# A convolution that adds its own input in the kernel tap, and predicated copies in place of masked adds

## The chip, the cores and the metric

The kernel runs on one core of one Trainium2 chip. A core has five engines, each with its own instruction stream: TensorE (PE, matrix products into the eight PSUM banks), VectorE (DVE), ScalarE (ACT), GpSimd (POOL) and SyncE (SP, which here mostly issues loads). They share the on-chip memory SBUF and meet through semaphores. The metric is the time of one execution on the device, in microseconds (us).

## The reference, cut to what matters

```python
# x: 32 x 64 x 1024 (batch, head or token, position or feature), float32
x = x + conv(x)        # per head: a causal convolution over 1024 positions with a kernel
                       # built from 64 states, plus x * D[head]; then zero behind length[batch]
x = x + einsum('bsi,boi->bso', x, weight1[ids1])     # per batch: its own 1024 x 1024 adapter
x = x + einsum('bij,bkj->bik', x, weight2[ids2])     # and a second one
gate = x @ Wg.T + low_rank(x, ids3)                  # 1024 -> 2752
up   = x @ Wu.T + low_rank(x, ids3)
x = x + (silu(gate) * up) @ Wd.T + low_rank(...)     # 2752 -> 1024
```

The convolution is `y = (k * u + u * D) * mask`, with `mask` one at the positions below the length of the batch and zero behind. So what goes on is `x + k*x + D*x` where the mask is one, and `x` itself where it is zero.

## The kernel before

**Layout.** The 32 batches are four chunks of eight (`NCK`, `BC`). `xs[c]` holds a chunk as 128 partitions by 8 feature tiles by 512 tokens. The convolution is computed for all four chunks at once, at the start. Its result for the first chunk goes into `xs[0]` in SBUF, that for the other three to a buffer `cd` in DRAM, from which `bring(c)` loads it later.

**The convolution** (`convolution`, about the first 140 us) handles 64 heads in 16 units of four; two units make a group, so there are eight groups g, and `period(g)` works on one. Inside it four streams run side by side, in an order that is written out by hand for DVE, ACT, POOL and SP (`period`, `run`, `spread`: a list of steps at which each piece is put among DVE's steps of the scan):

- ACT makes powers, 16 small products `m` for each unit (`products`, line 1602), in pieces of 8, 3 and 5 for one unit and 3 and 13 for the other; it also takes four results out of PSUM into SBUF (`xg<-pv`, line 1690), the turned powers (`e<-pt`, line 1664) and the taps (`ks<-pk`, line 1719).
- DVE sums the products into `zs` (two instructions for a unit, in `new_powers`), runs the scan over the states (`scan`: instructions `t` and `xg`), and takes the finished results out of the banks (`taken`). All DVE helpers go through `tt`, so their line is 1337.
- PE turns `zs` (`pt`), computes `pv` from it, the taps `pk`, and two parts of the result into the banks `py`: `direct` (from the taps) and `carried` (from the states, after the scan of that group has ended).
- The finished unit lies in two banks `py`, one for each `side`; each is 128 partitions by two heads by 4 chunks by 64. `taken` has three pieces: `masked(0)` and `masked(1)` multiply a whole bank by the mask into `tmp`, `added` adds the first chunk's part of `tmp` to `xs[0]` and stores the rest to `cd`.

The last group, g=7, has no further scan beside it. The banks are handed out in turn by `ps_tile`, eight in all, so a bank is used again eight allocations later.

**The adapters of the first chunk** follow, 16 of them (`adapter`, line 233). Their weights, 512 KB for each eighth of an adapter (k counts the eighths from 0), come through nine rotating buffers `w`, and 35 of them are `own`: loaded ahead into places in memory that the convolution leaves free, step by step (`places`, `fetch`: EARLY, then LATE, BETWEEN and LAST as groups end). `OWN_ENDS` says after how many adapters this memory is given up (`first.close()`), and `FIRST_RUN, RUN` which eighths are `own`. Between the adapters 10 and 13 stand small pieces of the next part: three `begin_rest(i)` (each loads one 512 KB block, runs eight matmuls and one ACT copy), and the first loads and products of the feed-forward part.

**The feed-forward part** (`ffn`) runs chunk by chunk, in three blocks, with sums of weights (`halves`, `quarters`, `sides`) that spare products. It loads `sums` and `parts` through the same nine buffers `w`, in order on SP's queue. The adapters of the next chunk are put between its pieces. `take(c)` adds the convolution's result to chunk c: eight DVE instructions of 128x512 (line 335) that `fill` hands out one by one, by an assumed cost, while the next chunk's first use of `xs[c]` is still to come.

Of the kernel before, what the change touches and what calls it, by code (L numbers as in the profile page):

```python
# [9 lines left out]
F32 = mybir.dt.float32  # L10
I32 = mybir.dt.int32
AF = mybir.ActivationFunctionType
ALU = mybir.AluOpType
# [6 lines left out]
P = 128  # L20
B, H, L = 32, 64, 1024
NS = 64
KT = L // P
NCK = 4
BC = B // NCK
TC = BC * H
# [6 lines left out]
MG = 2  # L33
NG = FM // MG
EARLY = 17
OWN_ENDS = 11
LATE = 5
BETWEEN = 4
LAST = 5
# [1 line left out]
WARM = 20  # L41
FIRST_ = 11
SECOND_ = 5
FIRST_RUN, RUN = 13, 11
MID = 6
ROTATING = 9
HA = 4
SEG = 2
TH = TC // 2
# [37 lines left out]
def kernel(  # L87
# [26 lines left out]
    nc = tc.nc  # L114
# [3 lines left out]
    wpool = ctx.enter_context(tc.tile_pool(name="wpool", bufs=ROTATING))  # L118
# [8 lines left out]
    def ps_tile(name):  # L127
        return psum.tile([P, 512], F32, tag="ps", name=name)

    cst = cpool.tile([P, CO_N], F32, tag="cst", name="cst")  # L130
# [11 lines left out]
    xs = [x_tile(0)]  # L142
    first = ExitStack()
# [6 lines left out]
    cd = dpool.tile([NCK - 1, P, H // HA, HA * KT * BC], F32, tag="cd", name="cd")  # L150
# [92 lines left out]
    def first_sides():  # L243


        for layer, b in list(layers(0))[:2]:
            acc, wts = begun[layer, b] = ps_tile(f"pa{layer}_{b}"), []
            for kt in range(KT if b == 0 else SECOND_):
                wts.append(next(stream))
                adapter_part(acc, wts[kt], kt, b * H, 0)  # L250
                yield
# [33 lines left out]
                ALU.add,  # L285
            )

    g0 = convolution(tc, cst, consts, xt, xf, ssm, eye, lens, xs[0], cd, ps_tile, fetch, places, (row_ids, rows_now), first, first_sides())
    for _ in before:
        pass  # L290

# [4 lines left out]
    later = deque()  # L296
# [28 lines left out]
    def take(c):  # L325
        n, half = H // 4, KT * BC // 2
        for q in range(4):
            t = came.pop(q)
            for i in (0, 1):

                def add(q=q, t=t, i=i):
                    rows_ = slice(i * half, (i + 1) * half)
                    xv = xs[c].rearrange("p k (b h) -> p (k b) h", h=H)
                    xv = xv[:, rows_, q * n : (q + 1) * n]
                    nc.vector.tensor_add(xv, xv, t.rearrange("p i k -> p k i")[:, rows_])

                later.append((1.0, add))

# [2 lines left out]
    def adapters(c):  # L343
        for layer, b in layers(c):
            yield adapter(layer, b)

    def rest_tile(i, name):
        wt = wpool.tile([P, KT, P], F32, tag="w", name=f"wr{i}_{name}")
        load = nc.sync.dma_start(wt.rearrange("p k f -> p (k f)"), wr[i])
        return wt, load.ins  # L350

    def rest_part(c, wt, ps, t0, t1):

        tokens = slice(t0, t1)
        for kt in range(KT):
            nc.tensor.matmul(  # L356
                ps[:, tokens],
                wt[:, kt, :],
                xs[c][:, kt, tokens],
                start=(kt == 0),  # L360
                stop=(kt == KT - 1),
            )

    layers0 = adapters(0)
    for _ in range(OWN_ENDS):
        next(layers0)
    first.close()

# [1 line left out]
    hpool = ctx.enter_context(tc.tile_pool(name="hpool", bufs=1, reuse_waits="tile"))  # L370
    gpool = ctx.enter_context(tc.tile_pool(name="gpool", bufs=2, reuse_waits="tile"))
# [26 lines left out]
    sums = [dpool.tile([7, P, 4 * QP], F32, tag=f"sums{i}", name=f"sums{i}") for i in range(2 * NG)]  # L398
    parts = [dpool.tile([4, P, 3 * QP], F32, tag=f"parts{i}", name=f"parts{i}") for i in range(2 * NG)]
    cols = []  # L400

    def columns(table, c, n, name, tags=("raw", "at"), behind=None):

# [29 lines left out]
    tms = {}  # L433
    for name in "gu":
        tms[name] = hpool.tile([P, 2 * H], F32, tag=f"tm_{name}", name=f"tm_{name}")
    rest1 = hpool.tile([P, TC], F32, tag="rest1", name="rest1")
    rest2 = hpool.tile([P, 2, TH], F32, tag="rest2", name="rest2")

    def pair(j):
        return slice(2 * R * j, 2 * R * (j + 1))  # L440
# [231 lines left out]
    def quarters(c, gi, g, o, xb, _, early, also=lambda: None):  # L672

        name = f"{c}_{gi}_{g}"
# [6 lines left out]
        def load(js):  # L681
            bs, as_ = [], []

            def home(j, n, name):
                pool, tag, bufs = (gpool, "wy", 2) if j == 2 else (wpool, "w", ROTATING)
                return pool.tile([P, n, KQ, P], F32, tag=tag, name=name, bufs=bufs)

            for j in js:
                t = home(j, 3, f"wb{j}_{name}")
                src = wq[2 * gi + g, raw[j]] if j in raw else parts[2 * gi + g][at_parts[j]]  # L690
                nc.sync.dma_start(t.rearrange("p i k f -> p (i k f)"), src)
                bs.append(t)
            for j in js:
                if j == 0:
                    t = gpool.tile([P, 4, KQ, P], F32, tag="wx", name=f"wa{j}_{name}", bufs=1)
                else:
                    t = home(j, 4, f"wa{j}_{name}")
                nc.sync.dma_start(
                    t.rearrange("p i k f -> p (i k f)"), sums[2 * gi + g][at_sums[j]]
                )  # L700
                as_.append(t)

            return [
                [b[:, 0], b[:, 1], a[:, 3], b[:, 2], a[:, 0], a[:, 1], a[:, 2]]
                for a, b in zip(as_, bs)
            ]
# [69 lines left out]
        add = nc.vector.tensor_add  # L776
        c11, c12, c21, c22 = quarter(o)
        l11, l12, _, _ = quarter(lt)
# [185 lines left out]
    def ffn(c, xb, sides0, others):  # L964
# [39 lines left out]
        tv = None  # L1004
        for block, (m0, m1) in enumerate(BLOCKS):
# [65 lines left out]
                flush()  # L1071
            if c == 0 and last:
                phase.close()
                qpool[0] = ctx.enter_context(
                    tc.tile_pool(name="qpool1", bufs=1, side="right", reuse_waits="tile")
                )
# [15 lines left out]
            for h in range(KH):  # L1092
                name = f"{c}_{block}_{h}"
                if last and h > 1 and more_come:
                    prepare(c + 1, "gu"[h - 2], ready)
                banks = [ps_tile(f"po{j}_{name}") for j in range(4)]

                home = {0: 0, 5: 1, 6: 2, 4: 3, 1: 4, 3: 5, 2: 6}
                pss = [banks[home[j] // 2][:, home[j] % 2 * TH :][:, :TH] for j in range(7)]
                for s0 in range(m0, m1, SEG):  # L1100
# [3 lines left out]
                    if block == 0:  # L1104
                        w = [wl[:, h, i] for i in range(3)]
                        tails = {1: (w[0], 0), 3: (w[1], 0), 4: (w[1], 1), 2: (w[2], 1)}
                    elif end and last:
# [3 lines left out]
                        w = [[wl[:, t, i, h * P : (h + 1) * P] for i in (0, 1)] for t in (0, 1)]  # L1111
# [69 lines left out]
            store()  # L1181
        return steps[0] if more_come else None

    def begin_rest(i):
        wt, ps = rest_tile(i, "first")[0], ps_tile(f"pr{i}_first")
        rest_part(0, wt, ps, 0, TH)
        nc.scalar.copy((rest1, rest2[:, 0], rest2[:, 1])[i][:, :TH], ps[:, :TH])
        return wt

    places_ = act_tile(0, "first").rearrange("p i m t -> p i (m t)")  # L1190
    other_ = apool.tile([P, MG, 4, TH], F32, tag="actd", name="actd_first")
    weight_places = [
# [34 lines left out]
        first_weight(m, 0)  # L1227
    xb, part = first_moving()
    next(layers0)
    begin_rest(1)  # L1230
    next(layers0)
    part(0, 2)
    begin_rest(2)
    next(layers0)
    tables = [
        columns(ag, 0, KT, "g_0", behind=loads[-1]),
# [22 lines left out]
        sides0 = None  # L1259


def convolution(tc, cst, consts, xt, xf, ssm, eye, lens, x0, cd, ps_tile, fetch, places, rows_now, first, sides):

# [7 lines left out]
    nc = tc.nc  # L1273
    NG_ = len(PAIRS)
    with ExitStack() as ctx:
# [18 lines left out]
        def load_u(g):  # L1294
            for u in range(PAIRS[g] // 2):
# [14 lines left out]

        shape = [P, NCK, 2, 2, KT * BC]
        work = [
            g0.tile(shape, F32, tag="tmp", name=f"work{i}", bufs=2).rearrange(
                "p c j s e -> p (c j s e)"
            )
            for i in (0, 1)
# [19 lines left out]
        def tt(o, a, b, op):  # L1336
            nc.vector.tensor_tensor(o, a, b, op)  # L1337
            return o
# [223 lines left out]
        nc.gpsimd.dma_start(kps[:, :P], zero)  # L1562

        lnf = g0.tile([P, B], F32, tag="lnf", name="lnf")
        mask = g0.tile([P, NCK, KT, BC], F32, tag="mask", name="mask")
        maskf = mask.rearrange("p c k b -> p (c k b)")
        nc.gpsimd.tensor_copy(lnf, ln)

        powers = {}

# [241 lines left out]
        def taken(g, u, c0=0, c1=NCK):  # L1812


            i_ = first_unit[g] + u
            ha = i_ * HA

            def masked(side):
                if c0 == 0 and side == 0:
                    tmps[i_] = g0.tile(shape, F32, tag="tmp", name=f"tmp{i_}", bufs=2)  # L1820
                tt(
                    tmps[i_][:, c0:c1, :, side].rearrange("p c j e -> p j c e"),
                    banks[g, u][side].rearrange("p j (c e) -> p j c e", c=NCK)[:, :, c0:c1],
                    maskf.rearrange("p (c e) -> p c e", c=NCK)[:, c0:c1]
                    .unsqueeze(1)
                    .to_broadcast([P, 2, c1 - c0, KT * BC]),
                    ALU.mult,
                )

            def added():  # L1830
                tmp = tmps[i_]
                if c0 == 0:
                    xv = x0.rearrange("p k (b h) -> p k b h", h=H)[..., ha : ha + HA]
                    tv = tmp[:, 0].rearrange("p j s (k b) -> p k b (j s)", b=BC)
                    tt(xv, xv, tv, ALU.add)
                if c1 == NCK:
                    queue = nc.scalar if g >= NG_ - 3 else nc.sync
                    queue.dma_start(
                        cd.rearrange("c p g e -> p c g e")[:, :, i_],
                        tmp[:, 1:].rearrange("p c j s e -> p c (j s e)"),  # L1840
                    )

            return (lambda: masked(0)), (lambda: masked(1)), added

        def masks():
            nc.vector.tensor_tensor(
# [407 lines left out]
```

## Time and profile before

| | |
|---|---|
| times of three runs | 2229.07, 2229.59, 2232.77 us |
| the profiled execution | 2230.71 us |
| its span | 2229.1 us |
| TensorE clock granted | 0.998 |
| PE busy | 2190.1 us (98%) |
| DVE busy | 1370.6 us (61%) |
| ACT busy | 423.8 us (19%) |
| POOL busy | 207.3 us (9%) |
| moved by DMA | 656.35 MB, 294 GB/s |

The profiled execution is 1.12 us above the median of the three, and 1.6 us lie around its span. A line of the timeline gives the start, the time to the end of the last of its instructions, the engine, the line of the kernel, output<-inputs, the shape, and in brackets how long the engine was idle before and what ended that. Successive instructions overlap a little, so an instruction's share of its engine is the distance of two starts, somewhat less than its own duration. In a line of waits stand the total, the number and the longest.

### The profile page before, as it was taken

Reading aid. Unit: us, or ns where it says so; the run is one execution under the profiler, and the core shown is the slowest. Engines: PE = TensorE matmul, PEld = TensorE weight load, DVE = VectorE, ACT = ScalarE, POOL = GpSimd, SP = SyncE. Lnnn points to the kernel's source line nnn. Section 1 sums busy time; section 2 is a strip of 40 time slices with the busy share of each in tenths; the row PEclk is TensorE's granted clock in tenths of the full one; section 3 lists DMA queues with packets and bytes.
Section 4 is the critical chain, followed back from the end, with each engine's and each line's share of the span. In section 5 each row is a group of like instructions: output and inputs, shape, how many; then the busy total and the mean of one; then the engine's idle time right before and its main releaser. Section 6 shows DMA issues by size and latency. Waiting matters only on the chain.

```text
span 2229.1 us, 53636 instructions
## 1 busy us (share of the span) xinstructions
PE 2190.1 (98%) x21488; PEld 1806.0 (81%) x21488; DVE 1370.6 (61%) x2995; ACT 423.8 (19%) x1042; POOL 207.3 (9%) x328
## 2 busy tenths in 40 slices
PE   7999999999999999999999999999999999999999
PEld 5765687877787896888689897788688988899998
DVE  8961386675367766565346666466336666576675
ACT  6800120110011121121012212122002212121220
POOL 1010031111011210000000111000000011000000
PEclk9999999999999999999999999999999999999999
DMA  8899998899979558799979848799989938384681
GB/s 316 272 346 396 404 376 297 331 361 362 361 285 370 195 199 312 286 361 357 354 289 362 279 145 319 275 350 363 353 294 359 329 107 290 121 291 177 215 277 41
DMA packets 204683, 656.35 MB, mean 294 GB/s; under 512 B 24066, under 2 KB 40834, under 8 KB 203922
## 3 DMA queue, kind: packets, MB, share of 16 engines
q1 hardware_dynamic: 173122, 565.84, 69.4%
q0 software_dynamic: 23392, 76.07, 9.1%
q10 hardware_dynamic: 7920, 11.01, 1.4%
q8 instruction: 169, 2.77, 0.5%
q14 instruction: 80, 0.66, 0.1%
HBM read 585.66 MB, written 67.17 MB: 293 GB/s over the span
## 4 chain that ended last, share of the span: by engine, by line
PE 86%; DVE 6%; DMA 5%; issue 3%; POOL 0%; ACT 0%; SPq 0%; POOLq 0%; DVEq 0%; ACTq 0%
PE pq L717 29%; PE po L1127 24%; PE pa L233 17%; PE pf L611 7%; PE pr L356 3%; DMA wa<-in_w 3%; PE pe L478 2%; DVE xg L1337 1%; DVE t L1337 1%; DMA sums<-kept 1%; PE pl_d L449 1%; DVE tmp L1337 1%; DMA wr_first<-in_wr 1%; PE pr_first L356 0%; DVE zs L1337 0%
## 5 line engine op out<-in xcount | busy, mean ns | idle before, releaser
L233 PE MATMUL pa<-wa,x 128*32 128x256 f32 x7632 | 431.7, 380 | 9.0 <-DMA wa<-in_w 9.0
L717 PE MATMUL pq<-xd,wa 128*128 128x128 f32 x3360 | 414.9, 275 | 0.4 <-DMA wa<-sums 0.4
L717 PEld LDWEIGHTS pq<-xd,wa 128*128 128x128 f32 x3360 | 394.6, 192 | 0.7 <-DMA wa<-sums 0.5
L233 PEld LDWEIGHTS pa<-wa,x 128*32 128x32 f32 x7632 | 240.6, 110 | 183.4 <-DMA wa<-in_w 17.7
L717 PE MATMUL pq<-xd,wb 128*128 128x128 f32 x2520 | 323.6, 276 | 0.0
L717 PEld LDWEIGHTS pq<-xd,wb 128*128 128x128 f32 x2520 | 300.5, 192 | 3.6
L262 DVE STREAM_TRANSPOSE y<-pa 128x512 f32<-128x512 f32 x64 | 45.9, 717 | 270.7 <-PE pa L233 266.9
L1127 PE MATMUL po<-act,wd 128*128 128x256 f32 x640 | 168.6, 386 | 0.0
L1127 PE MATMUL po<-actd,wd 128*128 128x256 f32 x640 | 164.2, 379 | 0.0
L1127 PE MATMUL po<-actd,s 128*128 128x256 f32 x640 | 164.2, 379 | 0.0
L504 DVE TENSOR_TENSOR s<-wd 128x256 f32<-128x256 f32 x80 | 33.8, 422 | 177.6 <-PE po L1127 177.5
L1127 PEld LDWEIGHTS po<-act,wd 128*128 128x128 f32 x640 | 117.8, 190 | 29.3 <-issue 12.5
L611 PE MATMUL pf<-xd,wf 128*128 128x256 f32 x576 | 135.5, 381 | 0.0
L1159 ACT COPY uo<-po 128x256 f32<-128x256 f32 x48 | 17.9, 372 | 616.3 <-PE po L1127 606.3
L1127 PEld LDWEIGHTS po<-actd,wd 128*128 128x128 f32 x640 | 121.6, 190 | 16.5
L1127 PEld LDWEIGHTS po<-actd,s 128*128 128x128 f32 x640 | 121.6, 190 | 16.5
L375 POOL DMA_INDIRECT bgu<-in_bgu,rows x44 | 44.6, 1014 | 968.3 <-PE pe L478 826.4
L611 PEld LDWEIGHTS pf<-xd,wf 128*128 128x128 f32 x576 | 108.7, 190 | 15.5
L611 PE MATMUL pf<-xd,s 128*128 128x256 f32 x480 | 114.5, 382 | 1.1 <-DVE up L652 1.0
L741 ACT COPY u<-pq 128x256 f32<-128x256 f32 x120 | 41.5, 345 | 367.0 <-PE pq L717 310.5
L611 PEld LDWEIGHTS pf<-xd,s 128*128 128x128 f32 x480 | 90.2, 190 | 16.9 <-DVE up L652 2.9
L746 DVE TENSOR_TENSOR u<-u,u 128x256 f32<-128x256 f32 x120 | 46.6, 388 | 73.9 <-ACT u L743 73.9
(275 smaller groups left out, 2762.8 us busy)
## 6 DMA issues: line engine op xcount, KB each, us to landing
wa<-in_w SPq DMA_DIRECT2D x477, 512.0 KB
wa<-sums SPq DMA_DIRECT2D x210, 512.0 KB
wb<-parts SPq DMA_DIRECT2D x120, 384.0 KB
wd<-in_wd SPq DMA_DIRECT2D x80, 512.0 KB
wb<-in_wq SPq DMA_DIRECT2D x90, 384.0 KB
sums<-kept POOLq DMA_DIRECT2D x30, 1024.0 KB, 7.7
wf<-in_wu SPq DMA_DIRECT2D x20, 512.0 KB
early<-in_w SPq DMA_DIRECT2D x17, 512.0 KB
```

The costliest lines, as they stand in the source:

```text
L233: nc.tensor.matmul(acc[i * S : (i + 1) * S, s * 256 : (s + 1) * 256], xs[lo // TC][:, kt, lo % TC + s * S : lo % TC + (s + 1) * S], wt[:, ...
L262: nc.vector.transpose(y, acc)
L356: nc.tensor.matmul(ps[:, tokens], wt[:, kt, :], xs[c][:, kt, tokens], start=(kt == 0), stop=(kt == KT - 1),)
L375: nc.gpsimd.indirect_dma_start(out=t, out_offset=None, in_=table, in_offset=bass.IndirectOffsetOnAxis(ap=at_, axis=0),)
L478: nc.tensor.matmul(ps[:, at_ * 2 * H : (at_ + 1) * 2 * H], bt[pair(j), g], tms[table][pair(j)], start=(g == 0), stop=True, skip_group_chec ...
L504: nc.vector.tensor_add(s1, a21, a22)
L611: nc.tensor.matmul(ps, ws[j][:, kt, :], xb[j][:, kt, :], start=start and kt == 0, stop=kt == KH - 1, skip_group_check=True,)
L717: nc.tensor.matmul(ps[:, to * TQ : (to + 1) * TQ], w[i][:, k, :], xb[:, j, SLOT[i], k, :], start=start and k == 0 and to == 0, stop=k == K ...
L741: nc.scalar.copy(u, pa)
L746: nc.vector.tensor_add(u, v, u)
L1127: nc.tensor.matmul(pss[j], *term, start=(s0 == m0 and i == 0 and home[j] % 2 == 0), stop=(end and i == len(terms) - 1 and not late), skip_ ...
L1337: nc.vector.tensor_tensor(o, a, b, op)
```

## The change

1. **Convolution.** The skip weight `dskip` gets one added (one POOL instruction), so the tap at zero distance holds D+1 and the banks hold result plus input. `masked` and `added` give way to `chosen` and `stored`. For each side, a predicated copy on DVE writes the bank's first chunk (128 by 2 heads by 64) into `xs[0]` where the mask, read as integers, is not zero; a plain copy takes the other three chunks (128 by 384) into `tmp`. The copy of side 0 is on DVE in groups 0 to 5, that of side 1 on ACT; in groups 6 and 7 both are on ACT. What is stored in `cd` is no longer masked.
2. **`take(c)`.** Each of the 24 adds of line 335 becomes a predicated copy of the same 128x512, with the mask; the cost that `fill` assumes goes from 1.0 to 1.2.
3. **Order.** `OWN_ENDS` goes from 11 to 12, `RUN` from 11 to 8: the `own` eighths are k = 2, 5, 8, 11, 13 to 20 and then every third from 22 (before: 13 to 23, then every third from 25). `begin_rest(1)` and `begin_rest(2)` move before the adapters 10 and 11; `begin_rest(0)`, which stood after adapter 10, now stands after adapter 11.
4. **Memory.** A pool `home` lives to the end and holds the mask and the two `tmp` buffers, in whose places `rest1` and `rest2` (now one tile `rests`) come later. A pool `rpool` with two buffers `wz`, from chunk 1 on, takes two of the eleven loads of a `quarters` step that went through the nine buffers `w`.

```diff
-OWN_ENDS = 11
+OWN_ENDS = 12
-FIRST_RUN, RUN = 13, 11
+FIRST_RUN, RUN = 13, 8
...
+    home = ctx.enter_context(tc.tile_pool(name="home", bufs=1))
+    mask = home.tile([P, NCK, KT, BC], F32, tag="mask", name="mask")
...
-                nc.vector.tensor_add(xv, xv, t.rearrange("p i k -> p k i")[:, rows_])
-                later.append((1.0, add))
+                    nc.vector.copy_predicated(
+                        xv,
+                        mask[:, c].rearrange("p k b -> p (k b)").bitcast(I32)[:, rows_]
+                        .unsqueeze(2)
+                        .to_broadcast([P, half, n]),
+                        t.rearrange("p i k -> p k i")[:, rows_],
+                    )
+                later.append((1.2, choose))
...
     layers0 = adapters(0)
-    for _ in range(OWN_ENDS):
+    for i in range(OWN_ENDS):
+        if i > OWN_ENDS - 3:
+            begin_rest(i - OWN_ENDS + 3)
         next(layers0)
     first.close()
...
-                pool, tag, bufs = (gpool, "wy", 2) if j == 2 else (wpool, "w", ROTATING)
+                pool, tag, bufs = wpool, "w", ROTATING
+                if j == 2:
+                    pool, tag, bufs = gpool, "wy", 2
+                elif j == 1:
+                    pool, tag, bufs = rpool[0], "wz", 2
...
-        maskf = mask.rearrange("p c k b -> p (c k b)")
+        maski = mask.rearrange("p c k b -> p (c k b)").bitcast(I32)
         nc.gpsimd.tensor_copy(lnf, ln)
+        nc.gpsimd.tensor_scalar(dskip, dskip, 1.0, None, ALU.add)
...
-            def masked(side):
-                if c0 == 0 and side == 0:
-                    tmps[i_] = g0.tile(shape, F32, tag="tmp", name=f"tmp{i_}", bufs=2)
-                tt(
-                    tmps[i_][:, c0:c1, :, side].rearrange("p c j e -> p j c e"),
-                    banks[g, u][side].rearrange("p j (c e) -> p j c e", c=NCK)[:, :, c0:c1],
-                    maskf.rearrange("p (c e) -> p c e", c=NCK)[:, c0:c1]
-                    .unsqueeze(1)
-                    .to_broadcast([P, 2, c1 - c0, KT * BC]),
-                    ALU.mult,
-                )
-
-            def added():
-                tmp = tmps[i_]
-                if c0 == 0:
-                    xv = x0.rearrange("p k (b h) -> p k b h", h=H)[..., ha : ha + HA]
-                    tv = tmp[:, 0].rearrange("p j s (k b) -> p k b (j s)", b=BC)
-                    tt(xv, xv, tv, ALU.add)
+            def chosen(side):
+                if c0 == 0:
+                    h = ha + side
+                    nc.vector.copy_predicated(
+                        x0.rearrange("p k (b h) -> p h (k b)", h=H)[:, h : h + 3 : 2],
+                        maski[:, : KT * BC].unsqueeze(1).to_broadcast([P, 2, KT * BC]),
+                        bank[side][:, :, 0],
+                    )
+                if c1 == NCK:
+                    if side == 0:
+                        tmps[i_] = home.tile(shape, F32, tag="tmp", name=f"tmp{i_}", bufs=2)
+                    copy = nc.vector.tensor_copy if side == 0 and g < NG_ - 2 else nc.scalar.copy
+                    copy(
+                        tmps[i_][:, 1:, :, side].rearrange("p c j e -> p j c e"),
+                        bank[side][:, :, 1:],
+                    )
```

## The prediction

> **What bounds the kernel now.** First I read the busy shares and PE's waits by stretch: they give all that a change outside PE can win. In the waits a line holds who waited, for what, the total, the number, the longest.
>
> ```profile
> PE 2190.1 (98%) x21488; PEld 1806.0 (81%) x21488; DVE 1370.6 (61%) x2995; ACT 423.8 (19%) x1042; POOL 207.3 (9%) x328
> ```
> ```profile
> PE py L1797 <- DVE xg L1337: 6.6, 7, 1.6
> ...
> PE pa L233 <- DMA wa<-in_w: 3.8, 8, 1.3
> PE pr_first L356 <- DMA wr_first<-in_wr: 0.6, 2, 0.3
> ...
> PE pa L233 <- DMA wa<-in_w: 5.2, 7, 1.7
> ```
>
> The first is from 0 to 146 us, the next two from 146 to 300, the last from 300 on. PE idles only 39 us (2229.1 less 2190.1). In the convolution it loses 6.6 to DVE's scan; up to 300 it loses 4.4 to loads. The table by stretch says what limits there (length, PE, PEld, DVE, ACT, POOL busy, clock, DMA share, GB/s):
>
> ```profile
> 100.00:120.00 20.00, 18.48 (x181) 14.96 (x178) 19.79 (x49) 13.20 (x47) 0.59 (x2) 1.00 0.71 237
> 120.00:140.00 20.00, 19.14 (x200) 14.30 (x199) 18.49 (x51) 1.06 (x2) 0.00 (x0) 1.00 1.00 353
> 140.00:300.00 160.00, 155.58 (x2370) 101.74 (x2372) 52.39 (x97) 11.72 (x22) 22.71 (x38) 1.00 1.01 399
> ```
>
> DVE is full up to 120; from 118 on, when the memory of the powers is given up and the late own weights are issued, the DMA is full, and PE still waits 0.29 for it at 250.57, at the last adapter pieces. So both chains matter: a convolution that ends later starts the full DMA later, and the 251 us mark moves with it.
>
> Then one group, g=3, in the timeline, DVE first, then ACT:
>
> ```profile
> 86.41 0.69 DVE L1337 TENSOR_TENSOR t<-xg,turn 128x512 f32<-128x512 f32 x1
> ...
> 88.36 0.68 DVE L1337 TENSOR_TENSOR tmp<-py,mask 128x512 f32<-128x512 f32 x1
> 88.97 0.68 DVE L1337 TENSOR_TENSOR t<-xg,turn 128x512 f32<-128x512 f32 x1
> 89.56 0.68 DVE L1337 TENSOR_TENSOR tmp<-py,mask 128x512 f32<-128x512 f32 x1
> ...
> 90.50 0.61 DVE L1337 TENSOR_TENSOR x<-x,tmp 128x256 f32<-128x256 f32 x1
> 91.02 0.42 DVE L1337 TENSOR_TENSOR xg<-xg,t 128x256 f32<-128x256 f32 x1
> ...
> 95.09 0.42 DVE L1337 TENSOR_TENSOR zs<-m 128x256 f32<-128x256 f32 x1
> ```
> ```profile
> 86.08 0.62 ACT L1664 ACTIVATE e<-pt 128x256 f32<-128x256 f32 x2
> 86.61 2.00 ACT L1602 ACTIVATE m<-zt,sz 128x64 f32<-128x64 f32 x8
> 90.42 0.54 ACT L1690 COPY xg<-pv 128x448 f32<-128x448 f32 x1 [1.80 <-PE pv L1682]
> 91.17 0.53 ACT L1690 COPY xg<-pv 128x448 f32<-128x448 f32 x1 [0.22 <-PE pv L1682]
> 91.60 0.83 ACT L1602 ACTIVATE m<-zt,sz 128x64 f32<-128x64 f32 x3
> 92.33 0.64 ACT L1664 ACTIVATE e<-pt 128x256 f32<-128x256 f32 x2
> 92.86 1.30 ACT L1602 ACTIVATE m<-zt,sz 128x64 f32<-128x64 f32 x5
> ```
>
> DVE's group runs 86.41 to 99.82 (13.41), back to back. ACT makes the 16 products for the `zs` at 95.09 in the pieces 8, 3, 5, done at 94.16: 0.93 spare.
>
> **The change part by part. DVE's work in the convolution** gets less. By distances of starts a `tmp` costs 0.60 and the add 0.52: a unit loses 2 x 0.60 + 0.52 = 1.72, a group 3.44. A unit gains two predicated copies of 128 elements and one copy of 384 from PSUM; the nearest rows for the copy are the `tmp` row of 384 elements of g=7 (four in 1.95: 0.48). For a predicated copy the cheapest row is `xg` 128x128 (0.22), the dearest I allow is the whole strided add of 256 (0.52); its write steps through `x` as that add does, so I take half of that add, 0.27. A group gains 4 x 0.27 + 2 x 0.48 = 2.04 and DVE's work falls by 1.40.
>
> **ACT's new copy turns that around.** The order of the changed kernel's instructions, readable before it runs, puts ACT's copy of side 1 after the first `e` pair and before the eight products, the second unit's after the second `e` pair and before the five. And each waits for DVE's predicated copy out of the same bank. ACT takes its instructions in order, so all of its group now hangs on DVE's second predicated copy. In g=3's terms, from the start of DVE's group: DVE's lead 1.95 (88.36 less 86.41), predicated copy 0.27, copy 0.48, `t` 0.60, predicated copy 0.35 to its end: 3.65. Passing on costs 0.10 (products ended at 60.01 and the waiting `zs` began at 60.11). ACT then needs: copy 0.39 (four 128x384 copies from PSUM took 1.63), eight products 1.92, two `xg` copies 0.86 (now without their 1.80 wait), three products 0.73, `e` pair 0.53, copy 0.39, five products 1.30: 6.12. So `zs` can start at 3.65 + 0.10 + 6.12 + 0.10 = 9.97, not 8.68, and from `zs` to the end DVE needs its old 4.73: a group of 14.70, 1.29 longer than before, though DVE has less to do. Behind the waiting ACT copy stand also the `xg` copies, for which DVE's next scan waits, and the second `e`, for which PE's `pv` waits (from 6.97 to about 8.2); both are inside the same 14.70. PE's work in a group, 11.84, is not the limit.
>
> By group: before 59.04 ACT is busy without a gap (19.60 of the 20 us from 40), so its two copies push it by 0.78, and the `zs` that already waits 0.38 at 60.11 comes at 60.89. From there the chain above (1.34 to the first predicated copy, then 1.70, 0.10, 6.12, 0.10) gives 70.25 for the `zs` of 68.17: +2.1. Groups 2, 3, 4 add 1.20, 1.29, 1.29: +5.9 where the full DMA begins. Group 5 has no products left, so DVE's saving counts, up to PE's wait of 0.51; group 6 the same, up to 0.35. PE leaves the convolution about 5.0 late.
>
> [...]
>
> **The loads.** They fall back with the memory of the powers: 5.9. `RUN` 8 instead of 11 shortens the run of own weights in which no rotating buffer comes free; that dip, 160 to 165, has a DMA share of 0.88, so at most 0.6 comes back. The two pieces of the remaining rows bring a 512 KB load, eight matmuls and one ACT copy each forward past adapters 10 to 12; bytes and PE work up to 251 are the same, and SP issues them in another order only: nothing. The load behind which SP stood from 208.5 to 214.85 is now issued one adapter later; it is used some 35 us after that: nothing. PE arrives 5.0 late, the loads 5.3: I take 5.2 at the 251 us mark.
>
> **`take`.** Sixteen of its 24 instructions are in chunks 1 and 2, where they have 2.0 us to spare. In chunk 0 they are on a full DVE:
>
> ```profile
> L335 DVE TENSOR_TENSOR x<-x,cv 128x512 f32<-128x512 f32 x8 | 7.9, 1059 | 0.0
> ```
> ```profile
> 348.71 0.28 DVE L461 TENSOR_TENSOR tv_d<-pl_d,cst 128x128 f32<-128x128 f32 x1
> ```
> ```profile
> 349.33 1.03 PE L1127 MATMUL po<-act,s 128*128 128x256 f32 x4
> ```
>
> The matmul at 349.33 needs the bank that line 461 frees: 0.3 spare. An add takes 0.97; a predicated copy between the `t` row of 512 without the stride (0.60, a gain that nobody waits for) and twice the add (8 x 0.97 - 0.3 = +7.5). Nearest is the add, with the same strided read; I take 0.1 more each: 0.8 - 0.3 = +0.5, of which waits for loads just behind (0.19, 0.94) may swallow 0.2: +0.3.
>
> **Buffers `wz`.** Loads may run about two ahead of before. The waits they could end are 1.72 at 1074.27, 1.60 at 1589.12 and 0.36 at 1354.83; the first two wait for a buffer that PE itself frees, in the same order: nothing, at best -3.7, and +0.5 if more loads stand ahead of those of the next step. The extra POOL addition precedes `pk` on an idle engine: nothing; late it would cost its own length. The end of g=7 sheds six DVE instructions behind PE's last product: nothing.
>
> **Sum.** 5.2 + 0.3 = 5.5 on 2230.71, the profiled execution: 2236.2. It stands 1.12 above the median, so 2235.1. What a measurement can tell from no change is about 0.2%, 4.46: up to 2234.05 counts as the same.
>
> **Rivals.** *The saving arrives* (the other side): ACT's copy holds up nobody, the wait lost among other slack. Then groups 2 to 4 give 1.40 each and 5 and 6 0.85: PE 5.0, loads 4.2 + 0.6; with +0.3, 2230.71 - 4.5 - 1.12 = 2225.1. For it: DVE is full in the convolution. Against: the arithmetic of one group. It decides if the `zs` starts before 8.68 into its group; even predicated copies at no cost leave it at 9.35.
>
> *Predicated copies are dear*: at 0.40 and 1.45 instead of 0.27 and 0.97, the convolution loses 0.26 more in each of four groups (1.0) and `take` 8 x 0.48 - 0.3 = 3.5 instead of 0.3: 2239.3; at twice the adds' price some 2244. No row speaks for or against.
>
> *The buffers end the late waits*: the 3.7 come back, 2231.4, the same. *The memory moves put a wait in* (`rests` is one tile, shared by ACT and DVE): 2 or 3 us, 2238; no row shows it.
>
> *The trace's DMA stage hides the convolution's delay* I hold for none: loads start late for the same reason.
>
> **How the numbers follow.** The forecast 0.50, own range 2232 to 2238, two thirds of it above 2234.05: 0.34 slower, 0.16 the same. Dear copies 0.22, slower. The saving 0.15, faster. Late waits ended 0.09, the same. Memory 0.04, slower. So slower 0.60, same 0.25, faster 0.15. The range of 2226 to 2241 leaves out about half of the saving rival and a third of the dear copies.
>
> **What would show it.** ACT's new copy with about 3 us of idle before it, ended by DVE's predicated copy, in each of groups 1 to 4; DVE waiting 2 to 3 us for products at the second `zs` pair; groups of 14.7; PE's waits for `xg` in the convolution near 12 instead of 6.6; first matmul after the 251 mark near 257; eight predicated copies at 1.1 each. Wrong it is if DVE stays back to back and groups shrink to 12.5, or if a predicated copy of 128 is far from 0.27.

## The result and the profile after

The changed kernel takes 2234.56 us (median of twelve runs, 2231.14 to 2236.89); the kernel before takes 2227.46 us over twelve runs (2225.12 to 2235.25). The two medians lie 7.1 us apart, the means 5.9; the ratio of the runs is 1.0025, with a 95% interval of 1.0015 to 1.0034: slower by about 5.6 us, between 3.3 and 7.6. The forecast was 2235.1, slower by 5.5 us. It stood on the three runs known then, whose median of 2229.59 is 2.1 us above that of the twelve, so of the two agreements the difference tells more than the total. The profiled execution took 2234.55 us with a span of 2232.7 us, 3.84 and 3.6 us more than the profiled execution before; as will be seen, two executions of the same kernel differ by as much in their late waits for loads, so the pair of profiles is read by stage, not by its total.

PE's work is the same; here are its busy time on the page, and those of its waits from 0 to 150 us, the convolution, that differ most from before (who waited, for what, total, number, longest):

```profile
PE 2189.3 (98%) x21488; PEld 1805.4 (81%) x21488; DVE 1366.0 (61%) x2987; ACT 430.6 (19%) x1062; POOL 206.4 (9%) x329
```
```profile
PE py L1813 <- DVE xg L1353: 7.6, 6, 1.7
PE pv L1698 <- ACT e L1680: 7.0, 6, 1.6
PE py L1797 <- DMA hk<-kp: 1.0, 1, 1.0
```

Before, PE lost 6.6 us to `xg` and 0.6 to `e`. Now it loses 7.6 and 7.0: it waits for DVE's scan as before, and also for ACT's second `e` pair, six times each. One group of the timeline shows why. First DVE, then ACT, of the changed kernel:

```profile
90.20 0.69 DVE L1353 TENSOR_TENSOR t<-xg,turn 128x512 f32<-128x512 f32 x1
...
92.15 0.72 DVE L1839 COPY_PREDICATED x<-mask,py 128x128 f32<-128x128 int32 x1
92.46 0.79 DVE L1848 COPY tmp<-py 128x384 f32<-128x384 f32 x1
93.17 0.68 DVE L1353 TENSOR_TENSOR t<-xg,turn 128x512 f32<-128x512 f32 x1
93.76 0.72 DVE L1839 COPY_PREDICATED x<-mask,py 128x128 f32<-128x128 int32 x1
94.07 1.12 DVE L1353 TENSOR_TENSOR xg<-xg,t 128x256 f32<-128x256 f32 x2
95.10 0.72 DVE L1839 COPY_PREDICATED x<-mask,py 128x128 f32<-128x128 int32 x1
...
100.72 0.43 DVE L1353 TENSOR_TENSOR zs<-m 128x256 f32<-128x256 f32 x1 [1.85 <-ACT m L1618]
```
```profile
90.09 0.62 ACT L1680 ACTIVATE e<-pt 128x256 f32<-128x256 f32 x2
94.56 0.48 ACT L1848 COPY tmp<-py 128x384 f32<-128x384 f32 x1 [3.85 <-issue]
94.93 2.02 ACT L1618 ACTIVATE m<-zt,sz 128x64 f32<-128x64 f32 x8
96.85 0.94 ACT L1706 COPY xg<-pv 128x448 f32<-128x448 f32 x2
97.69 0.83 ACT L1618 ACTIVATE m<-zt,sz 128x64 f32<-128x64 f32 x3
98.41 0.64 ACT L1680 ACTIVATE e<-pt 128x256 f32<-128x256 f32 x2
98.94 0.48 ACT L1848 COPY tmp<-py 128x384 f32<-128x384 f32 x1
99.30 1.32 ACT L1618 ACTIVATE m<-zt,sz 128x64 f32<-128x64 f32 x5
```

ACT has its first `e` pair done at 90.71, then stands for 3.85 us at its copy of side 1 until DVE's second predicated copy (93.76 + 0.72 = 94.48) has left that bank. Only then come the eight products that before ran at once. The five last products end at 100.62, and DVE, ready since 98.87, waits 1.85 for them. DVE's groups begin at 59.04, 74.93, 90.20, 105.45 and 120.73 (before: 59.04, 72.91, 86.41, 99.82, 113.23): a group takes 15.27 instead of 13.41. The page calls the wait "issue" here; the view of line 1839 names the two, with the time that others waited for it:

```profile
L1839 DVE COPY_PREDICATED x<-mask,py x32: 709/720/961, 46.6 to 149.0; 128x128 f32<-128x128 int32 x32
...
  ACT tmp L1848: 20.0, 8
```

Behind the convolution, the late own weights are issued at 126.47 (before 118.12, 8.35 later), and the last `carried` ends at 148.3 (before 140.5). Before, then after:

```profile
118.12 4.62 SPq L181 DMA_DIRECT2D late<-in_w  x5
138.49 2.00 PE L1797 MATMUL py<-xg,zs 64*128 64x64 f32 x32 [0.35 <-DVE xg L1337]
```
```profile
126.47 4.58 SPq L181 DMA_DIRECT2D late<-in_w  x5
144.15 4.17 PE L1813 MATMUL py<-xg,zs 64*128 64x160 f32 x64
```

The DMA is then full as before (a share of 1.03 from 148 to the mark, 1.01 from 140 before), and two dips that it had are filled. The table by stretch of ten us (the last two columns are DMA share and GB/s), before and after:

```profile
160.00:170.00 10.00, 10.00 (x192) 6.02 (x188) 1.41 (x2) 0.00 (x0) 0.00 (x0) 1.00 0.94 356
210.00:220.00 10.00, 9.69 (x128) 6.12 (x119) 1.41 (x2) 2.26 (x3) 0.00 (x0) 1.00 0.94 351
```
```profile
160.00:170.00 10.00, 10.00 (x192) 6.05 (x188) 1.75 (x3) 0.00 (x0) 0.00 (x0) 1.00 1.03 401
210.00:220.00 10.00, 10.00 (x136) 6.62 (x132) 1.41 (x2) 0.37 (x1) 3.82 (x7) 1.00 1.03 395
```

The matmuls `pf_first`, which stood at 251.57, stand at 257.75: 6.18 later. In `take` the eight predicated copies of 128x512 have the price of the adds:

```profile
L337 DVE COPY_PREDICATED x<-mask,cv 128x512 f32<-128x512 int32 x8 | 7.8, 1060 | 0.0
```

### The profile page after: what moved, and what is told of

The parts are those of the page before. It is cut to its first block, busy times and chain, and to the rows that moved or that the text cites. A ratio compares the mean times of both kernels' runs of the same rounds, so it can differ in the third digit from the quotient of the medians.

```text
span 2232.7 us, 53624 instructions
## 1 busy us (share of the span) xinstructions
PE 2189.3 (98%) x21488; PEld 1805.4 (81%) x21488; DVE 1366.0 (61%) x2987; ACT 430.6 (19%) x1062; POOL 206.4 (9%) x329
## 4 chain that ended last, share of the span: by engine, by line
PE 88%; DMA 4%; issue 1%; DVE 1%; ACT 0%; POOL 0%; SPq 0%; POOLq 0%; ACTq 0%; DVEq 0%
PE pq L739 30%; PE po L1152 24%; PE pa L233 18%; PE pf L629 8%; PE pr L364 3%; DMA wa<-in_w 3%; PE pe L496 2%; PE pl_d L467 1%; DMA sums<-kept 1%; DMA hk<-kp 0%; PE pl_g L467 0%; PE py L1813 0%; PE pl_u L467 0%; PE pr_first L364 0%; PE pf_first L1234 0%
## 5 line engine op out<-in xcount | busy, mean ns | idle before, releaser
L629 PEld LDWEIGHTS pf<-xd,s 128*128 128x128 f32 x480 | 90.2, 190 | 16.7 <-DVE up L670 2.7
```

Of the source, the lines that this page charges most:

```text
L629: nc.tensor.matmul(ps, ws[j][:, kt, :], xb[j][:, kt, :], start=start and kt == 0, stop=kt == KH - 1, skip_group_check=True,)
```

## The experiments

Three theories are tested. A: ACT's new copy waits for DVE, and what is queued behind it comes late. B: the predicated copies are dear, and the waiting is only their shadow. C: the new order and the pools cost time. In all of them "group" is the distance between two starts of DVE's group, 13.41 before, 15.27 after, and "the mark" is the first `pf_first`, 251.57 before, 257.75 after.

**e1: ACT's first copy behind the eight products.**

```diff
                     (4, lambda: made(ma, 8)),
+                    (4, lambda: later_copy.pop()()),   # ACT's copy of side 1, first unit
                     (4, lambda: inputs(g + 2, 0)),
```

> The changed kernel with one move: in groups 1 to 4 ACT's copy of side 1 of the first unit stands behind the eight products instead of ahead of them. Theory A (ACT's new copy waits for DVE's predicated copy, and the products behind it come late): the eight products run in the time that ACT now waits; from the start of DVE's group the copy starts at 4.37 as now, then 0.37 + 0.86 + 0.73 + 0.53 + 0.36 + 1.32, so the second zs pair can start near 8.7 instead of 10.54, DVE itself is ready at 8.6; a group takes 13.4 us instead of 15.27, ACT's wait at the copy falls from 3.9 to about 1.9, PE leaves the convolution about 7 us earlier, and the whole is 3 to 6 us faster than the changed kernel: near the kernel before (ratio 0.999 to 1.001). Theory B (the predicated copies are dear for DVE, and the waiting is only its shadow): the group stays at 15 us and the time at the changed kernel's, ratio 1.0025.

Measured: ratio to the kernel before 0.9994 (0.9985 to 1.0003), groups of 13.79, the mark at 252.22. Moving one instruction behind its neighbours takes the whole loss away. ACT and then DVE:

```profile
87.93 2.00 ACT L1618 ACTIVATE m<-zt,sz 128x64 f32<-128x64 f32 x8
91.81 0.48 ACT L1851 COPY tmp<-py 128x384 f32<-128x384 f32 x1 [1.87 <-DVE x L1840]
...
94.77 0.48 ACT L1851 COPY tmp<-py 128x384 f32<-128x384 f32 x1 [0.34 <-DVE x L1840]
```
```profile
96.55 0.43 DVE L1353 TENSOR_TENSOR zs<-m 128x256 f32<-128x256 f32 x1 [0.38 <-ACT m L1618]
```

The copy still waits for DVE, 1.87, but the eight products are done. That is theory A. The expected group of 13.4 was missed by 0.4: the second copy now waits 0.34, and DVE's wait at the `zs` is 0.38 instead of 1.85.

**e2: no copy on ACT in groups 0 to 5.**

```diff
-                    copy = nc.vector.tensor_copy if side == 0 and g < NG_ - 2 else nc.scalar.copy
+                    copy = nc.vector.tensor_copy if g < NG_ - 2 else nc.scalar.copy
```

> The changed kernel with the side-1 copy on DVE too in groups 0 to 5, so ACT waits for nothing of DVE there. Theory A: DVE's own 8.6 to the second zs pair grows by two copies of 0.71 to 10.0, its products are there at about 8.6; a group of 14.75, 0.5 less than the changed kernel's 15.27, and still 1.3 more than before: about 1 us faster than the changed kernel in total, ratio 1.001 to 1.002. DVE is back to back. Theory B (predicated copies dear): the two more copies on DVE make it worse, groups of 16.7, ratio 1.005.

Measured: ratio 1.0019 (1.0010 to 1.0028), groups of 14.32 (88.03 to 102.35), DVE back to back, no wait of DVE for products:

```profile
97.01 0.69 DVE L1353 TENSOR_TENSOR t<-xg,turn 128x512 f32<-128x512 f32 x1
97.62 0.42 DVE L1353 TENSOR_TENSOR zs<-m 128x256 f32<-128x256 f32 x1
```

More work for DVE makes the group shorter by 0.95: the wait costs more than the copies that it was meant to save. By theory B a group of 16.7 was expected. In total, though, e2 can't be told from the changed kernel, since the two intervals overlap. In its profile PE leaves the convolution at 145.4, 2.9 earlier than in the changed kernel, and yet the mark stands at 258.51. Up to there PE waits 4.6 for loads where the changed kernel has 2.0, and the granted clock is 0.50 from 254 to 256, where the mean of the changed kernel is 1.00 from 250 to 260 (over the whole executions 0.996 and 0.998).

**e3: only the order, `RUN` and the pools.** The convolution and the adds in `take` are those of the kernel before.

```diff
-                    nc.vector.copy_predicated(
...
+                tt(
+                    tmps[i_][:, c0:c1, :, side].rearrange("p c j e -> p j c e"),
...
+                    ALU.mult,
+                )
```

> The changed kernel with the convolution's masked multiplications and adds of the kernel before, and the adds in take; what is left of the change is the order around adapters 10 to 12, RUN, and the pools. Theory A (all the loss is in the convolution): groups of 13.4, the time of the kernel before or up to 2 us under it, ratio 0.999 to 1.000; waits for loads after 300 us about 2 us fewer than before. Theory C (order or pools cost): 2 to 5 us slower than before, groups of 13.4.

Measured: ratio 0.9992 (0.9983 to 1.0001), groups of 13.39 (86.33 to 99.72), the mark at 251.53. Theory C, a cost of several us, falls; whether this half of the change gains something is not settled by an interval that just takes in 1.

**e4: only the convolution and the predicated copies of `take`.**

```diff
-OWN_ENDS = 12
+OWN_ENDS = 11
-FIRST_RUN, RUN = 13, 8
+FIRST_RUN, RUN = 13, 11
```

(and `begin_rest`, `rests`, `rpool` and the cost that `fill` assumes as before)

> The kernel before with the convolution and the predicated copies of take of the changed kernel; order, RUN and pools as before. Theory A: groups of 15.27, PE leaves the convolution 7.8 us late, at least the changed kernel's loss, ratio 1.0025 to 1.0035. Theory C (order or pools cost): less than the changed kernel's loss, ratio 1.000 to 1.0015.

Measured: ratio 1.0032 (1.0020 to 1.0044), groups of 15.26 (89.94 to 105.20), the mark at 258.53. With e3, which has no loss, this puts the loss into the convolution; the instructions of `take`, the only other thing in e4, cost what the adds cost.

**e5: both of ACT's copies behind the products.**

```diff
                     (9, lambda: made(ma)),
+                    (9, lambda: later_copy.pop()()),   # and the second unit's
+                    (9, second[2]),
                     (9, lambda: inputs(g + 2, 1)),
```

> The changed kernel with both of ACT's copies in groups 1 to 4 moved behind the products that the second zs pair needs. Theory A (ACT's wait): the wait of 0.38 at the zs that was left with one copy moved goes, a group is what DVE needs alone, 13.35 to 13.45, as before; ratio to the kernel before 0.998 to 1.000. Since this is also what a group took before, it shows whether the predicated copies save DVE anything: at the price of 0.27 that was forecast a group would take 12.0 to 12.7, at the 0.67 that starts in the changed kernel suggest, 13.4.

Measured: ratio 0.9997 (0.9988 to 1.0006), groups of 13.30 (87.38 to 100.68), the mark at 251.47:

```profile
87.38 0.69 DVE L1353 TENSOR_TENSOR t<-xg,turn 128x512 f32<-128x512 f32 x1
...
95.96 0.42 DVE L1353 TENSOR_TENSOR zs<-m 128x256 f32<-128x256 f32 x1
...
100.68 0.69 DVE L1353 TENSOR_TENSOR t<-xg,turn 128x512 f32<-128x512 f32 x1
```

With no wait left for ACT at the `zs` of this group, DVE needs 13.30, and before it needed 13.41: the predicated copies save DVE next to nothing. The forecast had them saving 1.40 a group. So theory B has a share: dear copies do not make ACT wait, but they lengthen the wait, and they are why there was nothing to win.

**e6 and e7: one predicated copy a unit, from SBUF.** Whole banks go to `tmp`, side 0 by DVE, side 1 by ACT, so that a bank has one reader (`at_` is 0 there); e7 also moves the second unit's copy behind its products and its predicated copy later.

```diff
-                        tmps[i_][:, 1:, :, side].rearrange("p c j e -> p j c e"),
-                        bank[side][:, :, 1:],
+                            tmps[i_][:, at_:, :, side].rearrange("p c j e -> p j c e"),
+                            bank[side][:, :, at_:],
...
+                    nc.vector.copy_predicated(
+                        x0.rearrange("p k (b h) -> p (k b) h", h=H)[:, :, ha : ha + HA],
+                        maski[:, : KT * BC].unsqueeze(2).to_broadcast([P, KT * BC, HA]),
+                        tmps[i_][:, 0].rearrange("p j s e -> p e (j s)"),
+                    )
```

> Whole banks are copied to tmp, side 0 by DVE, side 1 by ACT (the first unit's behind the eight products), and one predicated copy of 256 elements a unit takes the first chunk from tmp to x; no bank is read by two engines in groups 0 to 5. Theory A: ACT waits only for PE's bank; DVE needs per unit 0.60 and a predicated copy of 256 of 0.6 to 0.8 instead of 1.72, a group 12.7 if products are in time; by ACT's order the zs pair can start near 8.4 (0.5 for the second unit's copy added to 7.85), so a group takes 12.8 to 13.2 and the time is 2 to 3 us under the kernel before, ratio 0.9985. Theory B (predicated copies dear wherever they read from): a group of 13.4 or more, ratio 1.000 or above.

> As the kernel with whole banks copied to tmp, and in groups 1 to 4 the second unit's copy on ACT stands behind the five products, with its predicated copy and store later in DVE's group. Theory A: nothing new lies ahead of the products, the zs pair can start near 7.9, DVE is ready at about 7.9 too: groups of 12.6 to 12.9, then limited by PE's 11.84 and DVE; the convolution ends 3 us earlier than before, the full DMA begins as much earlier; 2 to 4 us under the kernel before, ratio 0.998 to 0.999. Theory B: groups of 13.4.

Measured: 0.9995 (0.9986 to 1.0004) and 0.9995 (0.9985 to 1.0005), both short of what was expected. In e6 a group takes 13.39 (88.76 to 102.15): DVE's predicated copies wait 7.2 us in all for ACT's copies. In e7 it takes 13.09 (87.88 to 100.97), and from there 13.61: DVE waits 4.8 in all for products, and PE 2.6 for `uf` and 2.3 for `hk`, loads that stand on SP's queue behind the stores of `cd` (0.5 and 1.3 in e9, whose stores in groups 1 to 4 are on ACT's queue). The wait moved each time to the next thing that stood behind a copy.

**e8: the price of a predicated copy by itself.** This is e5, but the predicated copies write with unit stride into `tmp`. The first chunk goes on without the convolution's result.

```diff
-                        x0.rearrange("p k (b h) -> p h (k b)", h=H)[:, h : h + 3 : 2],
+                        tmps[i_][:, 0, :, side],
```

> As with both ACT copies later, but the predicated copies write 128 elements with unit stride into tmp instead of the strided places of x; the convolution is left out of the first chunk. The price alone: if the 0.72 us of a predicated copy (128 elements) come from the strided write, it falls to about 0.3 and groups to 12.2; if they come from the instruction itself or from its source in PSUM, it stays at 0.7 and groups at 13.4.

Measured, in one execution: 2224.92 us, groups of 12.58 (85.75 to 98.33), the mark at 247.85. In this group DVE waits 0.16 and 0.32 for products, so that its own work is near the expected 12.2. The view of the line gives shortest, median and longest duration in ns; here e8, with two rows of its timeline, and below it e6, whose copies write 256 elements, four neighbours at each place:

```profile
L1841 DVE COPY_PREDICATED tmp<-mask,py x32: 289/294/307, 47.2 to 138.9; 128x128 f32<-128x128 int32 x32
```
```profile
87.95 0.29 DVE L1841 COPY_PREDICATED tmp<-mask,py 128x128 f32<-128x128 int32 x1
88.15 0.55 DVE L1850 COPY tmp<-py 128x384 f32<-128x384 f32 x1
```
```profile
L1866 DVE COPY_PREDICATED x<-mask,tmp x14: 591/616/637, 50.7 to 133.8; 128x256 f32<-128x256 int32 x14
```

The same copy of 128 elements from the same bank takes 294 ns with unit stride and 720 ns into `x`, where each element lies 256 bytes from the last. The instruction is cheap; its place to write to is not. And 256 elements in groups of four take less than 128 single ones (616 against 720 ns), though that copy also reads from SBUF, so the two differ in more than the writing.

**e9, e11: all 16 products first.** e7, and ACT makes the first unit's 16 products before its first copy, the predicated copies come later, and ACT's queue issues the stores in groups 1 to 4.

```diff
-                    (4, lambda: made(ma, 8)),
+                    (4, lambda: made(ma)),
+                    (4, lambda: later_copy.pop()()),
                     (4, lambda: inputs(g + 2, 0)),
-                    (5, first[2]),
...
-                    (6, lambda: made(ma, 3)),
...
+                    (8, first[2]),
...
-                    (9, lambda: made(ma)),
+                    (9, lambda: later_copy.pop()()),
...
+                    (12, second[2]),
```

> As the kernel with whole banks copied to tmp and late second copies, and in groups 1 to 4 ACT makes all 16 products of the first unit at once, before its first copy and the xg copies; the predicated copies come later in DVE's group, and ACT's queue issues the stores to cd there instead of SP's. Theory A (what limits a group is what ACT has queued ahead of the products for the second zs pair): the products are done 4.8 after the start of DVE's group, the zs pair waits for nothing, a group is DVE's own 12.5; from group 2 to 5 that is 0.9 each, the 251 us mark comes 2 to 3 us earlier than before, ratio to the kernel before 0.998 to 0.999, the only version clear below 1. If groups are 12.5 and the 251 us mark still stands at 251.5, loads hold it (theory D), ratio 0.9995.

> The best version once more, beside the one with the order of before on the same chip: ratio 0.997 to 0.999, groups of 12.9, the 251 us mark near 248.7.

Measured: 0.9980 (0.9971 to 0.9989), and the second time 0.9987 (0.9979 to 0.9996). It beats the kernel before both times, and with it the changed kernel. Its groups take 12.90, DVE's second `zs` pair waits for nothing, and the mark stands at 248.66 and 247.36. ACT and DVE of e9:

```profile
87.53 3.92 ACT L1618 ACTIVATE m<-zt,sz 128x64 f32<-128x64 f32 x16
91.35 0.56 ACT L1854 COPY tmp<-py 128x512 f32<-128x512 f32 x1
```
```profile
93.30 0.69 DVE L1353 TENSOR_TENSOR t<-xg,turn 128x512 f32<-128x512 f32 x1
93.90 0.42 DVE L1353 TENSOR_TENSOR zs<-m 128x256 f32<-128x256 f32 x1
```

12.90 is 0.4 above the expected 12.5: the first `zs` pair of this group now waits 0.35 (at 87.18) for the 13 products that ACT makes last.

**e10: the convolution of e9 with order, `RUN` and pools of the kernel before.**

```diff
-OWN_ENDS = 12
+OWN_ENDS = 11
-FIRST_RUN, RUN = 13, 8
+FIRST_RUN, RUN = 13, 11
```

> The convolution of the best version (whole banks to tmp, all 16 products first) with order, RUN and pools of the kernel before. Theory A (the gain is the convolution's): groups of 12.9, late loads 1 to 2 us earlier than before, the 251 us mark 1 to 2 us earlier, since the two dips of the DMA at 160 and 210 us are back; ratio 0.9990. Theory C' (the order and pools bring most of it): ratio 0.9995 to 1.0005.

Measured: 0.9988 (0.9979 to 0.9997), groups of 12.87 (86.23 to 99.10), the mark at 249.17. The gain is the convolution's; beside e11's 0.9987 on the same chip the order and the pools add nothing that these runs can tell.

## Why the prediction was right, point by point

- **The wait of ACT for DVE**, the step that set the sign, is shown: by the wait in the trace, and by e1, where one instruction moved takes the loss away. By its parts: from ACT's copy to the `zs` 6.17 measured (79.30 to 85.47), 6.22 predicted; from the `zs` to the end of the group 4.73 and 4.73. DVE's lead up to ACT's copy was 4.37 (74.93 to 79.30) instead of 3.75, and that is 0.62 more; so the `zs` came 10.54 into the group, not 9.97, and a group took 15.27, not 14.70.
- **The step that was mis-sized is the predicated copy**, "0.27" and "0.35 to its end". Its neighbour starts 0.31 later, but it takes 0.72 to its end, and what follows pays: the copy of 384 takes 0.71 to the next start, not 0.48, and the `xg` pair behind the second one 1.03, not 0.67. The first unit shown costs DVE 0.31 + 0.71 + 0.31 + 0.36 = 1.69 where 1.72 went. The "fall by 1.40" was a fall of about 0.1, as e5 shows (13.30 against 13.41). What the wrong price added is the 0.62 by which the lead grew, or 0.57 a group, since ACT's part came out 0.05 shorter; the missing saving cost nothing, since DVE waits anyway. The forecast took the price from a strided add of 256 elements, halved. But that add writes 64 places of four neighbours, the predicated copy 128 places of one, and e5 against e8 shows that the places count (0.71 to 0.72 us against 0.29). A copy "far from 0.27" was one of the forecast's own signs of being wrong, and it came.
- **Group 1**: the `zs` predicted at 70.25 came at 70.20. Two errors cancel there: the first `zs` came at 60.27, not 60.89, since ACT's run of 32 products began at 41.09 instead of 41.62 and so took up most of what the two copies cost; and the lead was longer.
- **Groups 2 to 4** were forecast to add 1.20, 1.29 and 1.29; they added 1.77, 1.84 and 1.87, all by the lead. **Groups 5 and 6** gave nothing back, because DVE had no saving to give; in group 6 PE waits 0.98 for the taps `hk`. That wait seems to come with the order and the pools: e3 has it with the old convolution (1.1), and the kernel before, e4 and e10, with the old order, do not; but e2, with the new order, does not have it either. So PE leaves the convolution 7.8 late (last `carried` ends at 148.3, before at 140.5), where 5.0 was forecast.
- **The loads**: the late weights fell back 8.35, not 5.9, of which some 0.7 come with the order and the pools (118.85 in e3, 118.12 before), but from there to the mark it took 131.28 us instead of 133.45. The forecast allowed 0.6 for the dip at 160 and "nothing" for the load behind which SP stood; both dips are filled, about 0.9 us each. That `RUN` fills the first is not shown: e3, with the new order and the old convolution, still has it (a DMA share of 0.94 from 160 to 170), and e10, with the old order and a faster convolution, does not (1.02). The second is filled in e3 (1.03 from 210 to 220) and open in e10 (0.85), but filled in e4 too (1.02), where the convolution ends late and the order is the old one. So the mark moved 6.18, with 5.2 forecast: too little delay in the convolution, too little recovery in the loads.
- **`take`**: 0.3 forecast, nothing measured. The predicated copy of 512 has the add's price, 1060 and 1059 ns.
- **Behind the mark** the waits of 0.19 and 0.94 for loads are gone, so 5.05 is left. The other waits from there on are 4.6 in this execution of the changed kernel and 5.5 before. That the fewer waits are the work of the buffers `wz` can't be said. e9 and e11 are one kernel, and their waits there are

```profile
PE pa L233 <- DMA wa<-in_w: 2.4, 4, 1.4
```
```profile
PE pa L233 <- DMA wa<-in_w: 7.3, 8, 1.9
```

  Their spans are 2222.8 and 2226.5, though e11 was ahead by 1.3 at the mark. The forecast of "nothing" for `wz` stands untested beyond e10 against e11.
- **The rivals.** "The saving arrives" fell at its own condition: the `zs` came at 10.54, not before 8.68. "Predicated copies are dear" was right about the small ones and wrong about `take`; their share in the loss is the longer lead, some 0.57 in each of groups 1 to 4, which in group 1 the earlier `zs` hides. "The memory moves put a wait in" is against e3.
- **What would show it**: ACT's wait (3.3 to 3.9) and the mark near 257 came as described, and so did DVE's wait at the `zs`, a little shorter than the "2 to 3" that was said (1.85). "PE's waits for `xg` near 12" was wrong in form: they are 7.6, with another 7.0 at `pv`, since the second `e` pair is late too. The forecast had named that wait and then counted it nowhere by itself.
- **What was luck.** The sign and the way the loss comes about were forecast; that 5.5 meets 5.6 is luck in part. The convolution lost 2.8 more than was forecast (7.8, not 5.0), the stage of the loads gave 1.6 back where the forecast had 0.2 more lost, and from the mark on `take` and the waits behind it gave 1.13 back where 0.3 was to be lost. Together these nearly cancel (5.05).

## What to carry to other kernels

When work is shared between two engines that take their instructions in order, ask of each new instruction what it waits for, and then what stands behind it: here 0.4 us of work on an engine that was not the limit cost 1.5 us a group (15.27, against 13.79 in e1), because the products for the limiting engine stood behind it. The order of instructions showed this wait before anything ran (about 3 us forecast, 3.3 to 3.9 measured); put an instruction that waits for another engine behind the work that others need. And price an instruction by the row with the same pattern of writing, not by the row with the same name or number of elements: here a predicated copy of 128 took 294 ns in one pattern (e8) and 720 ns in the other.

## What the runs showed of the hardware

- A predicated copy of 128 elements from PSUM takes 294 ns with unit stride (e8) and 720 ns when each element is written 256 bytes from the last; the estimate from the two is (720 - 294) / 128, about 3.3 ns more for each single place. A copy of 256 elements into groups of four neighbours takes 616 ns (e6), and a DVE add of 256 with the same groups took 607 (the kernel before); both also read single elements 256 bytes apart. No run writes at a spacing between these, so its price there is not shown.
- The next DVE instruction starts 0.31 us after the start of such a strided copy, which takes 0.72, and then ends late itself: 0.79 for a copy of 384 that takes 0.55 in e8. The start of the next instruction is not the price.
- A predicated copy of 512 and an add of 512 take the same, 1060 and 1059 ns, with the same strided read.
- Two executions of one kernel (e9 and e11) differ by 4.9 us in their waits for loads after 262 us, at the same mean clock of 0.998. The eleven runs of e9 alone lie between 2222.45 and 2230.95 us, so a single pair of profiles can't show an effect of that size in those stages.
